# First layer's norm statistics moved to ScalarE, plain transposes of scaled rows, and an ordering edge on the scan's decay factors

## The chip, the core and the metric

The kernel runs on one core of one Trainium2 chip. The metric is the device time of one execution in microseconds (us); lower is better. Engines: PE is TensorE (PEld its weight loads), DVE is VectorE, ACT is ScalarE, POOL is GpSimd, and SP is SyncE, whose queue issues nearly all of the DMAs.

## The reference

Sixteen sequences (batches) of 512 tokens with 256 features, all in float32, pass through four residual layers: a state-space scan, a gated feed-forward layer whose operands go through a blockwise FP4 rounding, a linear attention, and the same feed-forward again. Each layer reads a layer norm of the running x.

```python
def _layernorm(x):                       # no gain, no bias
    return (x - mean(x)) / sqrt(var(x) + 1e-5)

# layer 1, per batch: d = 256 features, n = 16 states
x_in = xn @ w_in;  dt_low, Bm, Cm = split(x_in @ w_x)
dt = softplus(dt_low @ w_dt + b_dt) * 0.099 + 0.001
A = -exp(A_log)
for t in tokens:                         # the scan
    h = exp(dt[t] * A) * h + sum_d(dt[t] * A * u[t]) * Bm[t]
    y[t] = sum_n(h * Cm[t]) + Dp * u[t]
x = x + y
# layers 2 and 4: x + fp4_linear(silu(fp4_linear(xn, w_gate)) * fp4_linear(xn, w_up), w_down)
# layer 3: x + (causal linear attention with elu+1 features, 16 heads of 16) @ W_proj + b_proj
```

## The kernel before

**Tiling.** A batch is a tile `x` of 128 partitions by 4 chunks (`c`) by 256 features. Products want the features on the partitions, so each layer turns its normed tokens into `tT` (two halves `k` of 128 features by 512 tokens) through TensorE and copies the result out of PSUM on ScalarE.

**Stages.** Every batch passes through `scan` (layer 1: `prologue` for the next batch woven into `mamba` for this one), `ffn` 0 (tiles named `_f`), `attention`, and `ffn` 1 (`_g`). The stages are Python generators. Each `yield w` reports a weight, and `run_all` (L876) takes the stage whose pace is least, so that the scan of batch b, the first feed-forward of b-1, the attention of b-2 and the second feed-forward of b-3 are emitted interleaved. The constants `SCAN, FFN, ATTN` on L874 are the totals of the weights. The framework's scheduler then makes one queue for each engine out of the emitted program, by its own idea of durations; a queue is worked off in its order on the chip, and an instruction whose semaphore has not come holds everything behind it on that engine.

**The first layer's norm.** `front` (L446) computes the statistics: per chunk one `bn_stats` and one `bn_aggr` on DVE, then `inverse` (L400: a scale and shift on DVE, a power on POOL) gives `rstd`. The mean is never subtracted, because `centre` (L207) has taken it out of the weights. The three later norms get their statistics another way: the residual add on DVE leaves the row sum in `sums` (its `accum_out`), and `distances` (L394) squares x*(-256)+sum on ACT with the row sum in `dist`.

**`to_features`** (L422). Without `rstd` (the feed-forwards) it transposes with the identity, L429. With `rstd` (`front` and `attention`) it builds a diagonal matrix `diag` of one chunk's `rstd` on ACT (L435; two buffers, shared by both callers), and multiplies the raw rows by it on PE (L437), which transposes and scales at once: `x` is the stationary operand, `diag` the moving one.

**The scan.** `mamba` (L517) runs 16 steps for each batch. A step's decay factors live in one of `NBAR = 4` tiles `bar`. `spread` (L526) reads the step's dt from DRAM, broadcast over the 16 states, into a `bar` (L531, 511 KB, on SP's queue); it can start when the scan that last read that `bar` has ended. `decay` (L534) takes two exponentials and a square on ACT (L538, L541). The scan itself (L559) and the product with C (L563) are DVE's, the sum over the states (L569) is PE's. At step `at` the loop emits the decay of step `at + 1`, then the spread of step `at + 3`, then the scan of step `at`.

Names used later: L622 is the feed-forward's tanh on ACT, L623 and L624 the products behind it on DVE; L642 and L647 copy its transposed hidden tile `hqT` out of PSUM on ACT, and L651 is the down product on PE; L249 is the magnitude step of the FP4 rounding on ACT.

Of the kernel before, what the change touches and what calls it, by code (L numbers as in the profile page):

```python
# [10 lines left out]
F32 = mybir.dt.float32  # L11
BF16 = mybir.dt.bfloat16
AF = mybir.ActivationFunctionType
# [4 lines left out]
P = 128  # L18
# [14 lines left out]
def kernel(  # L33
# [385 lines left out]
            )  # L419
        return xn  # L420

    def to_features(pool, t, name, rstd=None):  # L422

        tT = pool.tile([P, ND, S], F32, tag="tT", name=f"tT_{name}", bufs=1)
        if rstd is None:
            for k in range(ND):
                pt = bank(f"pt_{name}_{k}")
                for c in range(NC):
                    nc.tensor.transpose(pt[:, ts(c, P)], t[:, c, ts(k, P)], ident)  # L429
                nc.scalar.copy(tT[:, k, :], pt)  # L430
            return tT
        pts = [bank(f"pt_{name}_{k}") for k in range(ND)]
        for c in range(NC):
            diag = small.tile([P, P], F32, tag="diag", name=f"diag_{name}_{c}")
            nc.scalar.activation(diag, ident, AF.Copy, scale=rstd[:, c : c + 1])  # L435
            for k in range(ND):
                nc.tensor.matmul(  # L437
                    pts[k][:, ts(c, P)], t[:, c, ts(k, P)], diag, start=True, stop=True
                )
        for k in range(ND):  # L440
            nc.scalar.copy(tT[:, k, :], pts[k])  # L441
        return tT
# [2 lines left out]

    def front(b, xt):  # L446

        stats = small.tile(
            [P, NC, nc.vector.BN_STATS_DIM], F32, tag="stats", name=f"st_m{b}"
        )  # L450
        mv = small.tile([P, NC, nc.vector.BN_AGGR_DIM], F32, tag="mv", name=f"mv_m{b}")
        for c in range(NC):
            nc.vector.bn_stats(stats[:, c, :], xt[:, c, :])
            nc.vector.bn_aggr(mv[:, c, :], stats[:, c, :])
        rstd = inverse(2, mv[:, :, 1], 1.0, f"m{b}")
        yield 2.4
        turned[b] = to_features(one, xt, f"m{b}", rstd)
        yield 1

    def prologue(b, xt):  # L460

        yield from front(b, xt)
        xnT = turned.pop(b)

        def from_xn(w, name):
            p = bank(f"{name}_{b}")
            for k in range(ND):
                nc.tensor.matmul(p, w[:, k], xnT[:, k, :], start=(k == 0), stop=(k == ND - 1))  # L468
            return p

        soft = one.tile([P, ND, S], F32, tag="soft", name=f"soft_{b}")
        dt = one.tile([P, ND, S], F32, tag="dt", name=f"dt_{b}")
        for e in range(ND):
            pz = from_xn(w_z_sb[:, :, ts(e, P)], f"pz{e}")
            nc.scalar.activation(soft[:, e, :], pz, AF.Abs, bias=b_dt_sb[:, e : e + 1])
            nc.scalar.activation(
                dt[:, e, :], pz, AF.Relu, bias=b_relu[:, e : e + 1], scale=DT_MAX - DT_MIN
            )  # L480
        yield 0.5
        nc.scalar.activation(soft, soft, AF.Tanh, scale=0.5)
        nc.scalar.activation(soft, soft, AF.Ln, bias=half_c, scale=0.5 * LN_C)
        nc.vector.scalar_tensor_tensor(dt, soft, DT_MIN - DT_MAX, dt, ALU.mult, ALU.add)

        dd = dram.tile([ND, 2, 32, 2, S], F32, tag="dt", name=f"dd_{b}")
        for e in range(ND):
            for q in range(4):
                nc.sync.dma_start(
                    dd[e, q // 2, :, q % 2, :], dt[32 * q : 32 * q + 32, e, :]  # L490
                )
        yield 1.5
        cm = one.tile([P, S], F32, tag="cm", name=f"cm_{b}", bufs=2)
        nc.scalar.copy(cm, from_xn(w_c_sb, "pcm"))
        yield 0.1

        while halfway[0] < b:
            yield 0
        u = one.tile([P, ND, S], F32, tag="u", name=f"u_{b}")
        for e in range(ND):  # L500
            nc.scalar.copy(u[:, e, :], from_xn(w_in_sb[:, :, ts(e, P)], f"pu{e}"))
        yield 0.5

        nc.vector.tensor_tensor(dt, dt, u, ALU.mult)
        pg = bank(f"pg_{b}")
        for k in range(ND):
            nc.tensor.matmul(
                pg, a_rep[:, k].rearrange("p n i -> p (n i)"), dt[:, k, :],
                start=(k == 0), stop=(k == ND - 1),
            )  # L510
        term = dt[:, 0, :]
        nc.scalar.copy(term, from_xn(w_b_sb, "pbm"))
        nc.vector.tensor_tensor(term, term, pg, ALU.mult)
        begun[b] = (u, dd, term, cm)
        yield 2

    def mamba(b, xt):  # L517
        u, dd, term, cm = begun.pop(b)

        inp = one.tile([P, 2, S], F32, tag="inp", name=f"inp_{b}")  # L520
        nc.scalar.copy(inp[:, 0, :], term)
        nc.gpsimd.tensor_copy(inp[:, 1, :], term)

        halves = small.tile([P, ND, NC], F32, tag="halves", name=f"halves_{b}")

        def spread(e, j, q0):  # L526

            bar = bars[state["bar"] % NBAR]
            state["bar"] += 1
            src = dd[e, q0 // 2, j * G8 : (j + 1) * G8, :, 1:S]  # L530
            nc.sync.dma_start(bar[:, :, 1:S], src.unsqueeze(0).to_broadcast([NS, G8, 2, S - 1]))  # L531
            return bar

        def decay(bar, e, j, q0):  # L534

            for i in range(2):
                g = 16 * e + 4 * (q0 + i) + j
                nc.scalar.activation(  # L538
                    bar[:, i, 1:S], bar[:, i, 1:S], AF.Exp, scale=a_col[:, g : g + 1]
                )  # L540
            nc.scalar.activation(bar[:, :, 1:S], bar[:, :, 1:S], AF.Square)  # L541
            return bar

        steps = [(e, j, q0) for e in range(ND) for j in range(4) for q0 in (0, 2)]
        sps = [spread(*steps[at]) for at in range(NBAR - 1)]
        ahead = decay(sps[0], *steps[0])
        for at, (e, j, q0) in enumerate(steps):
            bar = ahead
            if at + 1 < len(steps):
                ahead = decay(sps[at + 1], *steps[at + 1])  # L550
            if at + NBAR - 1 < len(steps):
                sps.append(spread(*steps[at + NBAR - 1]))
            if j == 0 and q0 == 0:
                py = ps_y.tile([P, S], F32, tag="y", name=f"py_{b}_{e}")
                nc.tensor.matmul(py, d_diag[:, e], u[:, e, :], start=True, stop=False)
                if e == ND - 1:
                    halfway[0] = b + 1
            h = one.tile([P, 2, S], F32, tag="hs", name=f"h_{b}_{e}_{j}_{q0}", bufs=3)
            nc.vector.tensor_tensor_scan(  # L559
                h.rearrange("p i t -> p (i t)"), bar.rearrange("p i t -> p (i t)"),  # L560
                inp.rearrange("p i t -> p (i t)"), 0.0, ALU.mult, ALU.add,
            )
            nc.vector.tensor_tensor(h, h, cm.unsqueeze(1).to_broadcast([P, 2, S]), ALU.mult)  # L563
            if q0 == 0:
                h0 = h
            else:

                for q in range(4):
                    nc.tensor.matmul(  # L569
                        py[32 * q : 32 * q + 32, :], red[:, j, :], (h0, h)[q // 2][:, q % 2, :],  # L570
                        start=False, stop=(j == 3),
                    )
            if j == 3 and q0 == 2:

                yT = one.tile([P, S], F32, tag="yT", name=f"yT_{b}_{e}")
                nc.scalar.copy(yT, py)
                pt = bank(f"pt_y_{b}_{e}")
                for c in range(NC):
                    nc.tensor.transpose(pt[:, ts(c, P)], yT[:, ts(c, P)], ident)
                for c in range(NC):  # L580
                    xc = xt[:, c, ts(e, P)]
                    nc.vector.scalar_tensor_tensor(
                        xc, pt[:, ts(c, P)], 1.0, xc, ALU.mult, ALU.add,
                        accum_out=halves[:, e, c : c + 1],
                    )
            yield 3.5

        stats["f", b] = sums, dist = summed(0, f"f{b}")
        nc.vector.tensor_tensor(sums, halves[:, 0, :], halves[:, 1, :], ALU.add)
        for c in range(NC):  # L590
            distances(xt, c, sums, dist)
        yield 2
# [80 lines left out]
    def attention(b, xs):  # L673
# [1 line left out]
        rstd = inverse(3, stats.pop(("a", b))[1], 1.0 / D**3, f"a{b}")  # L675
        stats["g", b] = summed(1, f"g{b}")
        yield 0.3
        xnT = to_features(att, xt, f"a{b}", rstd)
        yield 1


# [189 lines left out]
        nc.sync.dma_start(out[b].rearrange("(c p) d -> p c d", p=P), xs[b])  # L871


    SCAN, FFN, ATTN = 65.7, 40.2, 25.7  # L874

    def run_all(stages):  # L876

# [66 lines left out]
```

## Time and profile before

| | |
|---|---|
| median of 3 runs | 2773.36 us (2771.33 to 2779.51) |
| the profiled execution | 2774.32 us; span of its instructions 2772.6 us |
| DVE busy | 2432.1 us, 88% of the span |
| PE busy | 2418.5 us, 87% (PEld 1412.6 us, 51%) |
| ACT busy | 1504.5 us, 54% |
| POOL busy | 175.2 us, 6% |
| DMA | 165.00 MB, 60 GB/s over the span |
| granted TensorE clock | 0.942 of full speed |

Busy times of engines overlap; a row "line engine op out<-in xcount | busy, mean ns of one | idle before" says how long a group of instructions ran and how long its engine sat idle just before them, and what ended that. PE's busy time is modelled, and a float32 matmul shows as two records. Between about 700 and 2300 us the picture repeats with every batch: the store of dt to DRAM (L489) starts at 762.40 us for one batch and at 2226.07 us nine batches later, so a batch takes 162.6 us. After about 2450 us no scan is left, and only attention and feed-forward work of the last batches runs.

### The profile page before, as it was taken

The page shows a single profiled execution, that of the slowest core. Times are in us where ns is not written, and L with a number is a line of the kernel's source. Part 1 is how long each engine was busy: PE and PEld are TensorE (multiplying, and loading weights), DVE is VectorE, ACT ScalarE, POOL GpSimd, SP SyncE. Part 2 cuts the span into 40 slices and gives each one's busy share as a digit, 9 for nine tenths or more (in the row PEclk, how much of TensorE's full clock was granted, in tenths as well). Part 3 has the DMA queues.
Part 4 walks back from the last instruction along what each step waited for, and adds up shares of the span by engine and source line. Part 5 has one row for each costly group of instructions (what it writes and reads, how often), then busy time and mean ns, then how long its engine had stood idle before and what let it go on. Part 6 is the DMA issues. An engine that isn't in the chain of part 4 may idle for free.

```text
span 2772.6 us, 34094 instructions
## 1 busy us (share of the span) xinstructions
PE 2418.5 (87%) x12783; PEld 1412.6 (51%) x12783; DVE 2432.1 (88%) x3691; ACT 1504.5 (54%) x2910; POOL 175.2 (6%) x171
## 2 busy tenths in 40 slices
PE   5677889889898998989899898989989898898996
PEld 3134555455555555555555555545555554455664
DVE  7898898799899899989989999899999989887665
ACT  4776574465746556474555647455564645433332
POOL 2000000000001000000100000010000001000000
PEclk8788999999999999999999999999999999999998
DMA  5533222213113132221312232131322213200000
GB/s 144 129 99 84 61 54 50 73 46 91 46 38 88 42 80 50 78 60 38 84 46 77 53 77 61 39 84 41 81 54 65 73 38 73 50 1 8 8 1 15
DMA packets 97399, 165.00 MB, mean 60 GB/s; under 512 B 8689, under 2 KB 92626, under 8 KB 97234
## 3 DMA queue, kind: packets, MB, share of 16 engines
q1 hardware_dynamic: 95360, 161.77, 23.3%
q8 instruction: 100, 1.64, 0.3%
q10 hardware_dynamic: 1874, 1.06, 0.1%
q14 instruction: 65, 0.53, 0.1%
HBM read 146.02 MB, written 16.78 MB: 59 GB/s over the span
## 4 chain that ended last, share of the span: by engine, by line
DVE 39%; PE 37%; ACT 9%; DMA 8%; issue 4%; POOL 2%; SPq 0%; POOLq 0%; DVEq 0%; ACTq 0%
DVE h L559 15%; DMA bar<-dd 8%; PE pg_g L616 4%; PE pu_g L616 4%; DVE h L563 4%; PE po_g L651 4%; PE pg_f L616 3%; PE pu_f L616 3%; PE py L569 3%; ACT bar L538 2%; PE po_f L651 2%; DVE sm L736 2%; PE pz L468 2%; DVE v_f L245 2%; ACT bar L541 1%
## 5 line engine op out<-in xcount | busy, mean ns | idle before, releaser
L559 DVE TENSOR_TENSOR_SCAN h<-bar,inp 128x1024 f32<-128x1024 f32 x256 | 579.7, 2279 | 8.2 <-ACT bar L541 5.0
L538 ACT ACTIVATE bar<-bar,a_col 128x511 f32<-128x511 f32 x512 | 353.0, 717 | 319.6 <-DMA bar<-dd 291.9
L569 PE MATMUL py<-h,red 128*32 128x512 f32 x1024 | 295.8, 658 | 123.1 <-DVE h L563 122.0
L563 DVE TENSOR_TENSOR h<-h,cm 128x1024 f32<-128x1024 f32 x256 | 311.0, 1217 | 0.6
L541 ACT ACTIVATE bar<-bar 128x1022 f32<-128x1022 f32 x256 | 269.2, 1051 | 2.6
L651 PE MATMUL po_g<-wdT,hqT_g 128*128 128x256 f32 (+1 forms) x768 | 210.8, 420 | 36.8 <-ACT hqT_g L642 36.6
L651 PEld LDWEIGHTS po_g<-wdT,hqT_g 128*128 128x128 f32 (+1 forms) x768 | 146.7, 203 | 121.6 <-ACT hqT_g L642 70.4
L651 PE MATMUL po_f<-wdT,hqT_f 128*128 128x256 f32 (+1 forms) x768 | 198.5, 401 | 10.2 <-ACT hqT_f L642 10.2
L616 PE MATMUL pg_g<-wgT,tT_g 128*128 128x352 f32 x512 | 186.2, 486 | 0.8 <-DVE h_f L624 0.5
L651 PEld LDWEIGHTS po_f<-wdT,hqT_f 128*128 128x128 f32 (+1 forms) x768 | 137.5, 192 | 95.5 <-ACT hqT_f L647 29.0
L616 PE MATMUL pu_g<-wuT,tT_g 128*128 128x352 f32 x512 | 185.8, 487 | 0.3 <-DVE sm L736 0.3
L616 PE MATMUL pg_f<-wgT,tT_f 128*128 128x352 f32 x512 | 182.3, 479 | 0.1
L616 PE MATMUL pu_f<-wuT,tT_f 128*128 128x352 f32 x512 | 172.9, 460 | 4.5 <-DVE sm L736 2.7
L622 ACT ACTIVATE h_g<-pg_g 128x352 f32<-128x352 f32 x128 | 59.2, 462 | 209.5 <-PE pg_g L616 209.4
L736 DVE TENSOR_TENSOR sm<-psc,causal 128x512 f32<-128x512 f32 x256 | 163.9, 681 | 4.4 <-PE pn L760 3.5
L569 PEld LDWEIGHTS py<-h,red 128*32 128x32 f32 x1024 | 38.0, 111 | 227.2 <-DVE h L563 177.8
L774 POOL COPY dx<-den 128x256 f32<-128x256 f32 x64 | 42.3, 661 | 1435.3 <-PE pr L779 758.0
L249 ACT ACTIVATE big_f<-v_f 128x704 bf16<-128x704 f32 (+1 forms) x80 | 67.1, 839 | 119.1 <-DVE v_f L245 119.1
L616 PEld LDWEIGHTS pg_f<-wgT,tT_f 128*128 128x128 f32 x512 | 98.4, 198 | 65.4 <-issue 23.8
L616 PEld LDWEIGHTS pu_g<-wuT,tT_g 128*128 128x128 f32 x512 | 101.5, 201 | 58.9 <-issue 8.5
L623 DVE SCALAR_TENSOR_TENSOR h_g<-h_g,pg_g 128x352 f32<-128x352 f32 x128 | 65.0, 509 | 74.7 <-ACT h_g L622 74.6
L689 PE MATMUL pqk<-tT_a,w_qkv_sb 128*128 128x512 f32 x256 | 122.6, 616 | 8.2 <-ACT tT_a L441 8.2
(239 smaller groups left out, 4583.6 us busy)
## 6 DMA issues: line engine op xcount, KB each, us to landing
bar<-dd SPq DMA_DIRECT2D x256, 511.0 KB, 4.8
x<-in_L_attn_a_x_dram SPq DMA_DIRECT2D x16, 512.0 KB, 4.4
dd<-dt SPq DMA_DIRECT2D x128, 64.0 KB, 1.7
out_dram<-x SPq DMA_DIRECT2D x16, 512.0 KB, 4.9
w_qkv_sb<-in_L_attn_b_W_attn_dram ACTq DMA_DIRECT2D x1, 768.0 KB, 6.9
raw_d<-in_L_ffn_w_down_dram SPq DMA_DIRECT2D x1, 704.0 KB
raw_g<-in_L_ffn_w_gate_dram SPq DMA_DIRECT2D x1, 640.0 KB, 7.1
raw_u<-in_L_ffn_w_up_dram SPq DMA_DIRECT2D x1, 640.0 KB, 6.5
```

The costliest lines, as they stand in the source:

```text
L249: nc.scalar.activation(big, v, AF.Abs, scale=STEP)
L538: nc.scalar.activation(bar[:, i, 1:S], bar[:, i, 1:S], AF.Exp, scale=a_col[:, g : g + 1])
L541: nc.scalar.activation(bar[:, :, 1:S], bar[:, :, 1:S], AF.Square)
L559: nc.vector.tensor_tensor_scan(h.rearrange("p i t -> p (i t)"), bar.rearrange("p i t -> p (i t)"), inp.rearrange("p i t -> p (i t)"), 0.0, ...
L563: nc.vector.tensor_tensor(h, h, cm.unsqueeze(1).to_broadcast([P, 2, S]), ALU.mult)
L569: nc.tensor.matmul(py[32 * q : 32 * q + 32, :], red[:, j, :], (h0, h)[q // 2][:, q % 2, :], start=False, stop=(j == 3),)
L616: nc.tensor.matmul(pw[:, :HF], xqT[:, k, ts(c, P)], wT[:, k, cols], start=(k == 0), stop=(k == ND - 1),)
L622: nc.scalar.activation(hc, pg[:, :HF], AF.Tanh, scale=0.5)
L623: nc.vector.scalar_tensor_tensor(hc, hc, 1.0, pg[:, :HF], ALU.add, ALU.mult)
L651: nc.tensor.matmul(po[:, :D], hqT[:rows, r, :], wdT[:rows, r, :], start=(r == 0), stop=(r == NR - 1),)
L689: nc.tensor.matmul(pz, w_qkv_sb[:, k, ts(je, P)], xnT[:, k, :], start=(k == 0), stop=(k == ND - 1),)
L736: nc.vector.tensor_tensor(t, psc[g].rearrange("p (s t) -> p s t", t=P), causal.unsqueeze(1).to_broadcast([P, NH // 4, P]), ALU.mult,)
```

## The change

1. `front` takes no `bn_stats` and `bn_aggr` any more. For each chunk ACT runs a Copy with `accum_out` (the row sum) and then `distances`, as for the other norms; `inverse` divides by D**3. The weight of its first `yield` goes from 2.4 to 0.2, and `SCAN` from 65.7 to 63.5.
2. `to_features` with `rstd` scales whole rows (128x256) on ACT, chunk by chunk, into a tile `rows`, and PE transposes them with the identity. `rows` has no memory of its own: in `front` it shares the buffer of `soft`, in `attention` that of `ep`. The two `diag` buffers are gone.
3. In the scan, from the third step of a batch on, both exponentials of a step get an ordering edge behind the scan two steps ahead. The edge (`NoSync`) is one for the scheduler alone: it carries no semaphore, so it sets where the exponentials stand in ACT's queue and makes nothing wait on the chip by itself.

```diff
-    def to_features(pool, t, name, rstd=None):
+    def to_features(pool, t, name, rstd=None, tag=None):
 ...
+        rows = pool.tile([P, ND, S], F32, tag=tag, name=f"rows_{name}", bufs=1)
+        rows = rows.rearrange("p k s -> p (k s)")
         for c in range(NC):
-            diag = small.tile([P, P], F32, tag="diag", name=f"diag_{name}_{c}")
-            nc.scalar.activation(diag, ident, AF.Copy, scale=rstd[:, c : c + 1])
+            row = rows[:, ts(c, D)]
+            nc.scalar.activation(row, t[:, c, :], AF.Copy, scale=rstd[:, c : c + 1])
             for k in range(ND):
-                nc.tensor.matmul(
-                    pts[k][:, ts(c, P)], t[:, c, ts(k, P)], diag, start=True, stop=True
-                )
+                nc.tensor.transpose(pts[k][:, ts(c, P)], row[:, ts(k, P)], ident)
 ...
     def front(b, xt):
-        stats = small.tile(...)
-        mv = small.tile(...)
+        sums, dist = summed(0, f"m{b}")
         for c in range(NC):
-            nc.vector.bn_stats(stats[:, c, :], xt[:, c, :])
-            nc.vector.bn_aggr(mv[:, c, :], stats[:, c, :])
-        rstd = inverse(2, mv[:, :, 1], 1.0, f"m{b}")
-        yield 2.4
-        turned[b] = to_features(one, xt, f"m{b}", rstd)
+            nc.scalar.activation(squares, xt[:, c, :], AF.Copy, accum_out=sums[:, c : c + 1])
+            distances(xt, c, sums, dist)
+        rstd = inverse(2, dist, 1.0 / D**3, f"m{b}")
+        yield 0.2
+        turned[b] = to_features(one, xt, f"m{b}", rstd, "soft")
 ...
-        def decay(bar, e, j, q0):
+        def decay(bar, e, j, q0, behind=None):
             for i in range(2):
 ...
+                exp = nc.scalar.activation(bar[:, i, 1:S], bar[:, i, 1:S], AF.Exp, ...)
+                if behind is not None:
+                    tc.add_manual_dep(exp.ins, behind.ins.name, <NoSync>, reason="dt lands")
 ...
+        scans = []
         for at, (e, j, q0) in enumerate(steps):
             bar = ahead
             if at + 1 < len(steps):
-                ahead = decay(sps[at + 1], *steps[at + 1])
+                ahead = decay(sps[at + 1], *steps[at + 1],
+                              behind=scans[at - 1] if at >= 1 else None)
 ...
-            nc.vector.tensor_tensor_scan(
+            step = nc.vector.tensor_tensor_scan(
 ...
+            scans.append(step)
 ...
-        xnT = to_features(att, xt, f"a{b}", rstd)
+        xnT = to_features(att, xt, f"a{b}", rstd, "ep")
 ...
-    SCAN, FFN, ATTN = 65.7, 40.2, 25.7
+    SCAN, FFN, ATTN = 63.5, 40.2, 25.7
```

More of the change, by code (lines that the diff above doesn't have):

```diff
@@ L446, in front @@
     def front(b, xt):
[L448 to L451, printed above, removed]
+        sums, dist = summed(0, f"m{b}")
         for c in range(NC):
-            nc.vector.bn_stats(stats[:, c, :], xt[:, c, :])
-            nc.vector.bn_aggr(mv[:, c, :], stats[:, c, :])
-        rstd = inverse(2, mv[:, :, 1], 1.0, f"m{b}")
-        yield 2.4
-        turned[b] = to_features(one, xt, f"m{b}", rstd)
+            nc.scalar.activation(squares, xt[:, c, :], AF.Copy, accum_out=sums[:, c : c + 1])
[3 more added lines that the diff above has]
+        turned[b] = to_features(one, xt, f"m{b}", rstd, "soft")
         yield 1
@@ L469, in from_xn @@
             return p
-        soft = one.tile([P, ND, S], F32, tag="soft", name=f"soft_{b}")
+        soft = one.tile([P, ND, S], F32, tag="soft", name=f"soft_{b}", bufs=1)
         dt = one.tile([P, ND, S], F32, tag="dt", name=f"dt_{b}")
@@ L532, in spread @@
             return bar
-        def decay(bar, e, j, q0):
+        def decay(bar, e, j, q0, behind=None):
             for i in range(2):
                 g = 16 * e + 4 * (q0 + i) + j
-                nc.scalar.activation(
+                exp = nc.scalar.activation(
                     bar[:, i, 1:S], bar[:, i, 1:S], AF.Exp, scale=a_col[:, g : g + 1]
                 )
+                if behind is not None:
+                    tc.add_manual_dep(
+                        exp.ins, behind.ins.name,
+                        mybir.DependencyInfo(
+                            mybir.DependencyClass.NoSync, mybir.DependencyReason.DATA
+                        ),
+                        reason="dt lands",
+                    )
             nc.scalar.activation(bar[:, :, 1:S], bar[:, :, 1:S], AF.Square)
@@ L549, in mamba @@
             if at + 1 < len(steps):
-                ahead = decay(sps[at + 1], *steps[at + 1])
+                ahead = decay(
+                    sps[at + 1], *steps[at + 1],
+                    behind=scans[at - 1] if at >= 1 else None,
+                )
             if at + NBAR - 1 < len(steps):
```

## The prediction

> **What bounds the kernel now.** I read the page's busy times first, then its chain, then one steady stretch, then the waits, and last the chain in order of time.
>
> ```profile
> PE 2418.5 (87%) x12783; PEld 1412.6 (51%) x12783; DVE 2432.1 (88%) x3691; ACT 1504.5 (54%) x2910; POOL 175.2 (6%) x171
> DVE 39%; PE 37%; ACT 9%; DMA 8%; issue 4%; POOL 2%; SPq 0%; POOLq 0%; DVEq 0%; ACTq 0%
> ```
>
> Two engines are nearly full, and the chain changes between them. The odd entry is DMA with 8% of 2772.6 us, about 222 us, although the queues are mostly empty. A steady batch (columns: us, then PE, PEld, DVE, ACT, POOL busy) says the same without start and end:
>
> ```profile
> 727.00:886.00 159.00, 143.86 (x784) 84.22 (x784) 145.02 (x225) 91.89 (x178) 10.27 (x9) 0.97 0.26 63
> ```
>
> DVE is busy 91% of it, PE 90%, ACT 58%. So no more than 9% can come from waits here; the rest must be work taken off DVE and PE. The waits of all engines (total us, times, longest):
>
> ```profile
> ACT bar L538 <- DMA bar<-dd: 291.9, 149, 7.4
> DVE h_g L623 <- ACT h_g L622: 74.6, 60, 5.2
> DVE h_f L623 <- ACT h_f L622: 53.9, 35, 5.4
> PE po_g L651 <- ACT hqT_g L642: 36.6, 37, 3.0
> ACT diag_a L435 <- PE pt_a L437: 31.8, 28, 3.5
> ACT diag_m L435 <- PE pt_a L437: 18.6, 13, 2.2
> ```
>
> ACT stands 292 us before exponentials whose dt has not landed; DVE and PE stand behind ACT's tanh and copies. The chain shows how the first makes the second (start, us, what):
>
> ```profile
> 787.36 2.21 DVE h L559
> 789.59 4.86 DMA bar<-dd
> 794.49 0.05 issue
> 794.54 1.33 ACT bar L538 x2
> 795.87 0.48 ACT hqT_g L642
> 796.35 0.04 issue
> 796.39 3.85 PE po_g L651 x12
> ```
>
> A scan ends and frees a `bar`; its refill takes 4.86 us; two exponentials stand in ACT's queue for that refill, and the hidden tile's copy, which has nothing to do with them, stands behind them, and PE behind the copy. This comes about three times in each steady batch.
>
> **Part 1: the statistics.** What goes from DVE and what its nearest substitute costs on ACT:
>
> ```profile
> L453 DVE BATCH_NORM_STATS2 st_m<-x 128x6 f32<-128x256 f32 x64 | 24.3, 402 | 0.1
> L454 DVE BATCH_NORM_AGGREGATE mv_m<-st_m 128x2 f32<-128x6 f32 x64 | 10.3, 167 | 0.0
> L395 ACT ACTIVATE squares<-x,sum_g 128x256 bf16<-128x256 f32 x64 | 32.4, 506 | 19.0 <-DVE x L388 12.7 <-DVE half_g L236 5.5
> L395 ACT ACTIVATION_READ_ACCUMULATOR squares<-x,sum_g 128x1 f32 x64 | 12.1, 188 | 0.0
> ```
>
> DVE loses 24.3 + 10.3 = 34.6 us. DVE's time is its work plus its idle time, so this comes off in full unless idle time replaces it. ACT gains, for 64 chunks, two passes with accumulator: 2 x (32.4 + 12.1) = 89 us. ACT has 46% idle, which covers them; uncovered, they would cost up to 89. The new dependence is DVE's `var_m` (L403) waiting for the last `distances`; everything on DVE stands behind it. The other three norms have that wait already, and DVE lost 2.4 us to it in 48 times. Bounds 0 to 16 x 1.4 us (one chunk's two passes) = 22; I take 5. At the start POOL is busy with two powers of 5.4 us until 18 us and takes `rstd_m` only then, which hides batch 0's sums; batch 1's stand among ACT's setup copies in the built order: 0 to 5.6 us, I take 3. The yields fall together with `SCAN`, so the pace of the stages stays.
>
> The Trainium skill (ScalarE: Activation LUTs, Rules for kernel authors) speaks against this part: adds and multiplies belong on VectorE, not ScalarE. A chunk costs 0.57 us on DVE here and 1.39 us on ACT, so the trace agrees on the direction. By that rule the move would lose 64 x 0.82 = 52 us wherever ACT is what all wait for.
>
> **Part 2: rows and transposes.** Before and after by the nearest rows:
>
> ```profile
> L437 PE MATMUL pt_a<-diag_a,x 128*128 128x128 f32 x256 | 51.6, 366 | 14.0 <-ACT diag_a L435 13.8
> L437 PE MATMUL pt_m<-diag_m,x 128*128 128x128 f32 x256 | 37.3, 288 | 8.1 <-ACT diag_m L435 7.0 <-ACT wgT L313 0.7
> L429 PE MATMUL pt_f<-ident,xn_f 128*128 128x128 f32 x128 | 18.7, 292 | 2.7 <-DVE xn_f L253 2.5 <-ACT ep L696 0.2
> ```
>
> A product with `diag` shows as two records, a transpose as one: 128 products make 256 records in `pt_a`, while 128 transposes make 128 in `pt_f`. 256 products took 51.6 + 37.3 = 88.9 us; 256 transposes at 18.7/128 = 0.146 us take 37.4. PE loses 51.5 us. PE holds 37% of the chain, so I count 0.37 x 51.5 = 19 us; bounds 0 and 51.5. A scaled row is 128x256 with a scale by partition, like `ko` (L722, 499 ns) against `diag`'s 400: 128 x 0.1 = 13 us more on ACT, covered as above. In return no row waits for PE to hand back one of two `diag` buffers, 31.8 + 18.6 + 5.8 = 56 us of ACT's waits. Sharing buffers costs nothing: `soft` and `ep` were last read about 100 us before (L484 and L834 run near 1413 us, the next norm near 1540), and what writes them next needs `tT` anyway.
>
> At 1376 to 1380 us, where `pt_a` runs, the granted clock is 0.71 and `pt_a` takes 201 ns a record against 146 for `pt_m`; transposes of `pt_h_g` amid matmuls (1426 to 1429 us) have 1.00. The Trainium skill (TensorE: Matmul & The Clock Gate, Part 4: PE-mode transpose) says that transposes do not count as activity for releasing the clock. By that, part 2 would gain 256 x 0.055 = 14 us less of PE's time; the second window speaks against it for short runs of transposes.
>
> **Part 3: the ordering edge.** It carries no semaphore. In the built program the median count of ACT instructions between a step's refill and its first exponential goes from 5 to 18. To see whether that is enough I summed, for each step, the DVE work (by these rows' durations) that must have passed between the scan that frees the `bar` and the last DVE result that ACT has already waited for when it reaches the exponential. Where it is under 5.4 us (4.8 to land, 0.54 to issue) ACT may stand. That is so in 238 of 256 steps before and in 69 after, and what is missing sums to 938 and 197 us. ACT really stood 292; in proportion, 61 are left (estimate), so 79% go. Most of those left are steps 1, 6 and 9 of each batch.
>
> What it is worth is less than ACT's 292 or the chain's 222, since DVE mostly works meanwhile. I laid DVE's idle stretches between 100 and 2450 us (197 us) against ACT's 149 waits, each with the 3.5 us behind it (two exponentials, square, one more): 63 us coincide, and 119 of PE's 268. DVE's idle time is the one that adds to its work, so I take 0.79 x 63 = 50. Bounds: 0 (other waits fill the holes) and 119 (PE's).
>
> **The sum.** -34.6 (DVE work) - 50 (waits) - 19 (PE) + 5 (`var_m`) + 3 (start), and + 2.6 because ACT's 102 us more work is 7% more, taken on the 37 us that DVE waits for ACT's rounding step `big` (24.0 for L251 in `v_g`, 13.2 in `v_f`): -93. The profiled execution took 2774.3 us, 1.7 more than its span and 1 more than the median of the runs: 2681, so 2680.
>
> **Rivals.**
> *More than the sum.* Both full engines are relieved in the same places, and a queue in which ACT no longer stands lets PE run ahead as well. For it: PE's 119 us and the 56 us of waits for `diag`. Against: DVE's work alone is 2397 us, with about 15 idle at the start and 104 after 2450 us, so 2516 is the floor. With PE's 119 in place of the 50: 2681 - 69 = 2612.
> *Only the work goes.* ACT stands elsewhere instead: `h_g` already waits 209 us for PE's `pg_g`, which no edge changes. Then the 50 us stay: 2731; if PE's 19 stay too, 2750. This is also the case in which the edge does nothing on the chip.
> *Slower: the decay comes too late.* Exponentials queued behind the scan two ahead also stand behind ACT's waits for PE, and then the scan waits for the whole decay, 0.72 + 0.61 + 0.95 = 2.28 us of the chain. Before, the scan lost 5.0 us to ACT in all: the decays were far ahead. In the built program the DVE work between what ACT has waited for and the scan falls from a median of 24 to 12.5 us, and is under 5.6 in a sixteenth of the steps. It outweighs the gain once 93/2.28 = 41 of 224 steps wait in full; with 60 the time is 2680 + 137 = 2817. The 12.5 us speak against it.
> *Slower: ACT becomes the bound.* If all of ACT's 102 us lie on the chain, the time is 2680 + 102 = 2782; it decides from 93 us on. ACT's 58% in the steady batch speaks against it. The rule of the Trainium skill named in part 1 (ScalarE: Activation LUTs, Rules for kernel authors) would have it so.
>
> **How the numbers follow.** The sum 0.57, more 0.2, only work 0.14, too late 0.06, ACT bound 0.03. The time is that of the sum, 2680. The range, 2600 to 2755, takes in "more" and "only work" and leaves the two slower cases out, with part of the first rival's low tail. About 0.3% (8 us) is what a measurement of this kernel can tell from no change: faster 0.88, same 0.04 (the upper end of "only work", the lower of "too late"), slower 0.08.
>
> **What would show it.** ACT's wait for DMA before the exponentials near 60 us instead of 292, and DMA under 3% of the chain; DVE busy near 2397, PE near 2367, ACT near 1607; the rows of the tanh waits (74.6 and 53.9) down by a third; the scan's wait for ACT under 20 us; a batch in 156 to 157 us instead of 162.6. The prediction is wrong if the scan's wait for `bar` exceeds 90 us, or if DVE's idle time between 100 and 2450 us stays near 197 with the DMA waits gone.

## The result, and the profile after

The changed kernel takes 2725.68 us (median of 4 runs, 2721.27 to 2727.22) against 2773.54 us of the kernel before beside it: a ratio of 0.982, 95% interval 0.980 to 0.984. That is 48 us faster; 93 were forecast. The profiled execution took 2721.27 us with a span of 2719.5 us, 53.1 less than before. The page's busy times and its chain:

```profile
PE 2372.8 (87%) x12527; PEld 1379.8 (51%) x12527; DVE 2404.1 (88%) x3563; ACT 1560.4 (57%) x3166; POOL 216.5 (8%) x171
DVE 46%; PE 31%; ACT 10%; issue 6%; POOL 4%; DMA 2%; DVEq 0%; SPq 0%; POOLq 0%; ACTq 0%
```

DMA has nearly left the chain (8% to 2%), and POOL's share has doubled (2% to 4%). DVE is busy 28.0 us less, and the span less that busy time, DVE's idle time, goes from 340.5 to 315.4 us: 28.0 of work and 25.1 of idle time make the 53.1. The waits after (total us, times, longest):

```profile
ACT bar L537 <- DMA bar<-dd: 46.4, 22, 4.7
DVE h_g L635 <- ACT h_g L634: 39.1, 26, 5.2
DVE h_f L635 <- ACT h_f L634: 22.3, 21, 2.3
DVE x L388 <- PE pro L826: 28.5, 18, 2.5
DVE h L570 <- PE py L581: 27.5, 12, 2.9
PE py L581 <- DVE h L575: 76.8, 45, 6.7
PE pt_a L440 <- ACT rows_a L438: 71.8, 38, 5.1
```

The last four were not shown before, and stood there like this:

```profile
DVE x L388 <- PE pro L814: 8.7, 8, 1.9
DVE h L559 <- PE py L569: 2.1, 2, 1.4
PE py L569 <- DVE h L563: 122.0, 53, 7.1
PE pt_a L437 <- ACT diag_a L435: 13.8, 3, 6.2
```

ACT's wait for dt fell from 291.9 to 46.4 us, and with it DVE's two waits for tanh, from 128.5 to 61.4. At the same time DVE waits 45 us more for PE (`pro` and `py`); PE waits 58 us more for the scaled rows, and 45 us less for the scan's product (`py`). The steady stretch, in the columns of a window, between the stores of dt of the same nine batches; first before, then after:

```profile
762.40:2226.07 1463.67, 1327.79 (x7147) 776.38 (x7147) 1341.28 (x2053) 837.56 (x1621) 92.44 (x81) 0.97 0.25 62
```

```profile
741.55:2181.55 1440.00, 1302.01 (x7004) 763.65 (x7003) 1326.01 (x1981) 867.83 (x1765) 116.90 (x81) 0.95 0.25 63
```

A batch now takes 160.0 us instead of 162.6: 24 us of the gain are here, 21 before the seventh batch's store, 9 after the sixteenth's. In the steady stretch DVE lost 15 us of work and only 8 of idle time. The groups that the change made, and the power they wait for:

```profile
L440 PE MATMUL pt_a<-ident,rows_a 128*128 128x128 f32 x128 | 39.1, 421 | 73.2 <-ACT rows_a L438 71.8
L440 PE MATMUL pt_m<-ident,rows_m 128*128 128x128 f32 x128 | 22.3, 325 | 5.6 <-ACT rows_m L438 5.6
L451 ACT ACTIVATE squares<-x 128x256 bf16<-128x256 f32 x64 | 26.0, 406 | 1.6 <-DMA x<-in_L_attn_a_x_dram 1.1
L395 ACT ACTIVATE squares<-x,sum_m 128x256 bf16<-128x256 f32 x64 | 32.1, 501 | 0.9
L405 POOL TENSOR_TENSOR rstd_a<-var_a,neg_half 128x4 f32<-128x4 f32 x16 | 45.1, 2818 | 73.0 <-DVE var_a L403 73.0
```

The same power took 1924 ns on average before. Where the new wait lies is seen in one norm of the attention, in the chain in order of time:

```profile
1027.64 0.09 DVE var_a L403
...
1027.80 2.92 POOL rstd_a L405
...
1030.75 0.51 ACT rows_a L438
1031.26 0.49 ACT squares L395 x2
1031.75 0.40 ACT rows_a L438
1032.15 0.40 ACT squares L451 x2
1032.55 0.40 ACT rows_a L438
1032.94 0.49 ACT squares L395 x2
1033.44 0.40 ACT rows_a L438
1033.84 0.61 ACT bar L537
1034.45 0.55 ACT tT_a L442
...
1035.04 3.59 PE pqk L701 x4
```

Three things follow one another: a power of 2.92 us; the four scaled rows, with part 1's passes for the first layer's statistics between them; and an exponential ahead of the copy of `tT`, which now waits for nothing. PE stands until the first rows come, and then gets them in pairs; here is its timeline, with the idle time before each piece in brackets:

```profile
1031.31 0.69 PE L440 MATMUL pt_a<-ident,rows_a 128*128 128x128 f32 x2 [5.12 <-ACT rows_a L438]
...
1035.04 3.58 PE L701 MATMUL pqk<-tT_a,w_qkv_sb 128*128 128x512 f32 x4 [0.46 <-ACT tT_a L442]
```

5.12 us idle, and then four records of `pqk` (two products) in 3.58 us. At the same place before, PE had the scan's sums (`py`) to work on ahead of `pt_a` and between its groups, and twelve records of `pqk` took 5.42 us:

```profile
1048.98 1.92 PE L569 MATMUL py<-h,red 128*32 128x512 f32 x2 [3.99 <-DVE h L563]
...
1056.13 5.42 PE L689 MATMUL pqk<-tT_a,w_qkv_sb 128*128 128x512 f32 x12 [0.58 <-ACT tT_a L441]
```

### The profile page after: what moved, and what is told of

The parts are those of the page before. It is cut to its first block, busy times and chain, and to the rows that moved or that the text cites. A ratio compares the mean times of both kernels' runs of the same rounds, so it can differ in the third digit from the quotient of the medians.

```text
span 2719.5 us, 33632 instructions
## 1 busy us (share of the span) xinstructions
PE 2372.8 (87%) x12527; PEld 1379.8 (51%) x12527; DVE 2404.1 (88%) x3563; ACT 1560.4 (57%) x3166; POOL 216.5 (8%) x171
## 4 chain that ended last, share of the span: by engine, by line
DVE 46%; PE 31%; ACT 10%; issue 6%; POOL 4%; DMA 2%; DVEq 0%; SPq 0%; POOLq 0%; ACTq 0%
DVE h L570 11%; DVE h L575 5%; PE po_f L663 3%; PE pg_f L628 3%; PE pqk L701 3%; DVE sm L748 3%; PE pu_f L628 2%; PE pg_g L628 2%; DMA bar<-dd 2%; PE py L581 2%; DVE v_f L245 2%; PE pu_g L628 2%; PE po_g L663 2%; POOL rstd_a L405 2%; POOL rstd_f L405 2%
## 5 line engine op out<-in xcount | busy, mean ns | idle before, releaser
L570 DVE TENSOR_TENSOR_SCAN h<-bar,inp 128x1024 f32<-128x1024 f32 x256 | 580.5, 2279 | 35.9 <-PE py L581 27.5
L537 ACT ACTIVATE bar<-bar,a_col 128x511 f32<-128x511 f32 x512 | 347.8, 718 | 48.9 <-DMA bar<-dd 46.4
L581 PE MATMUL py<-h,red 128*32 128x512 f32 x1024 | 267.6, 673 | 76.8 <-DVE h L575 76.8
L663 PE MATMUL po_f<-wdT,hqT_f 128*128 128x256 f32 (+1 forms) x768 | 205.6, 412 | 13.2 <-ACT hqT_f L654 13.2
L663 PE MATMUL po_g<-wdT,hqT_g 128*128 128x256 f32 (+1 forms) x768 | 200.4, 404 | 14.7 <-ACT hqT_g L654 14.7
L663 PEld LDWEIGHTS po_g<-wdT,hqT_g 128*128 128x128 f32 (+1 forms) x768 | 138.9, 194 | 95.5 <-ACT hqT_g L659 36.9
L701 PE MATMUL pqk<-tT_a,w_qkv_sb 128*128 128x512 f32 x256 | 141.2, 700 | 7.0 <-ACT tT_a L442 7.0
L249 ACT ACTIVATE big_g<-v_g 128x704 bf16<-128x704 f32 (+1 forms) x80 | 67.6, 845 | 122.3 <-DVE v_g L245 122.1
L634 ACT ACTIVATE h_g<-pg_g 128x352 f32<-128x352 f32 x128 | 57.9, 460 | 129.7 <-PE pg_g L628 129.4
L654 ACT COPY hqT_f<-pt_h_f 128x512 f32<-128x512 f32 (+1 forms) x128 | 50.5, 424 | 135.8 <-PE pt_h_f L650 133.9
L628 PEld LDWEIGHTS pu_f<-wuT,tT_f 128*128 128x128 f32 x512 | 97.3, 190 | 54.7 <-DVE h_g L635 2.1
```

Source lines behind the costliest of these rows:

```text
L249: nc.scalar.activation(big, v, AF.Abs, scale=STEP)
L537: exp = nc.scalar.activation(bar[:, i, 1:S], bar[:, i, 1:S], AF.Exp, scale=a_col[:, g : g + 1])
L570: step = nc.vector.tensor_tensor_scan(h.rearrange("p i t -> p (i t)"), bar.rearrange("p i t -> p (i t)"), inp.rearrange("p i t -> p (i t)" ...
L581: nc.tensor.matmul(py[32 * q : 32 * q + 32, :], red[:, j, :], (h0, h)[q // 2][:, q % 2, :], start=False, stop=(j == 3),)
L628: nc.tensor.matmul(pw[:, :HF], xqT[:, k, ts(c, P)], wT[:, k, cols], start=(k == 0), stop=(k == ND - 1),)
L634: nc.scalar.activation(hc, pg[:, :HF], AF.Tanh, scale=0.5)
```

## The experiments

The kernel before ran beside every group; its median there was 2770.3 to 2774.3 us, and each ratio is against it.

### The three parts alone and in pairs

**Theories.** A: the ordering edge earns most, and the other parts give some of it back. B: only the work taken off earns. Six kernels have the remaining combinations of the three parts.

**edge_only**: part 3 on the kernel before.

```diff
-                ahead = decay(sps[at + 1], *steps[at + 1])
+                ahead = decay(sps[at + 1], *steps[at + 1],
+                              behind=scans[at - 1] if at >= 1 else None)
```

> Part 3 alone, on the kernel before: the ordering edge on the exponentials; statistics on DVE and the diagonal matmuls as before. Theory A (the edge earns most, and other parts give some of it back): ACT's wait for bar from DMA falls from 292 us to under 70, DVE's idle time between 100 and 2450 us falls by 40 to 60 us, and the time is 2715 to 2735 us. Theory B (only the work taken off DVE and PE earns; the holes that the edge closes open elsewhere): the wait for DMA falls as in A, but the time stays within 10 us of 2773.

2745.53 us, 0.990 (0.989 to 0.992). ACT's wait fell to 47.0 us as both theories had it, but both times are missed, and DVE's idle time between 100 and 2450 us fell by 13 us and not by A's 40 to 60.

**rows_only**: part 2 alone, on the kernel before.

```diff
-            diag = small.tile([P, P], F32, tag="diag", name=f"diag_{name}_{c}")
-            nc.scalar.activation(diag, ident, AF.Copy, scale=rstd[:, c : c + 1])
+            nc.scalar.activation(row, t[:, c, :], AF.Copy, scale=rstd[:, c : c + 1])
...
-                nc.tensor.matmul(pts[k][:, ts(c, P)], t[:, c, ts(k, P)], diag, start=True, stop=True)
+                nc.tensor.transpose(pts[k][:, ts(c, P)], row[:, ts(k, P)], ident)
```

> Part 2 alone: scaled rows and plain transposes for both callers; statistics on DVE, no edge. PE busy falls by 46 to 52 us in both theories. Theory A: 2745 to 2765 us (PE holds 37% of the chain before, 19 us). Theory B: all that the change earned comes from the work of parts 1 and 2, so here about half of the 48 us: 2745 to 2755.

2775.77 us, 1.001 (0.999 to 1.003): above both ranges, and PE's busy time fell by 21.6 us in place of 46 to 52.

**stats_only**: part 1 alone, on the kernel before.

```diff
-            nc.vector.bn_stats(stats[:, c, :], xt[:, c, :])
-            nc.vector.bn_aggr(mv[:, c, :], stats[:, c, :])
+            nc.scalar.activation(squares, xt[:, c, :], AF.Copy, accum_out=sums[:, c : c + 1])
+            distances(xt, c, sums, dist)
...
-        yield 2.4
+        yield 0.2
...
-    SCAN, FFN, ATTN = 65.7, 40.2, 25.7
+    SCAN, FFN, ATTN = 63.5, 40.2, 25.7
```

> Part 1 alone: sums and distances on ACT, SCAN 63.5, first yield 0.2; diagonal matmuls and no edge. DVE busy falls by 28 to 35 us in both theories. Theory A: ACT already stands 292 us for DMA, and 90 us more work in the same queue eats most of it: 2755 to 2780. Theory B: 2738 to 2748, the work of DVE in full.

2770.51 us, 1.000 (0.998 to 1.002), as A has it; DVE's busy time fell by 17.8 us, less than the 28 to 35 of both.

**rows_stats**: the changed kernel without the edge.

```diff
-                    behind=scans[at - 1] if at >= 1 else None,
+                    behind=None,
```

> Parts 1 and 2 without the edge (the changed kernel with no edge given). Theory A: ACT's wait for DMA is back at 250 to 300 us and the time 2750 to 2775. Theory B: the wait is back but the time stays at 2720 to 2735, as with the edge.

2799.56 us, 1.010 (1.008 to 1.011): slower than before, and above both ranges; ACT's wait is back at 233.5 us.

**edge_rows**: parts 2 and 3, which is rows_only with the edge of edge_only.

```diff
+                              behind=scans[at - 1] if at >= 1 else None)
```

> Parts 2 and 3 together, statistics still on DVE. The runs so far: the edge alone 0.990 of before, rows alone 1.001, statistics alone 1.000, rows and statistics 1.010, all three 0.982. Theory C (the work that each part takes off is small and is worth something only where the queues' order lets it; the edge repairs the order that parts 1 and 2 spoil): 2725 to 2740 us, more gained than by the edge alone. Theory D (the parts add up and the rest is chance of the order): the edge's 27 us and nothing more, 2740 to 2752.

2751.38 us, 0.993 (0.990 to 0.995): D's range, not C's.

**edge_stats**: parts 1 and 3, the changed kernel with `diag` put back.

```diff
-            nc.scalar.activation(row, t[:, c, :], AF.Copy, scale=rstd[:, c : c + 1])
+            diag = small.tile([P, P], F32, tag="diag", name=f"diag_{name}_{c}")
+            nc.scalar.activation(diag, ident, AF.Copy, scale=rstd[:, c : c + 1])
```

> Parts 1 and 3 together, with the diagonal matmuls. Theory C: 2720 to 2740 us, since DVE's 28 us of work come off once ACT does not stand for DMA. Theory D: 2740 to 2752 us.

2733.57 us, 0.987 (0.985 to 0.989): C's range, not D's.

All eight combinations side by side. The times are medians; the rest is from one profiled execution of each. DVE's idle time is the span less its busy time; the last three columns are ACT's wait for dt, PE's wait at `pt_a` for its operand, and PE's wait at `py` for the scan's product:

| parts | us (median) | DVE busy | DVE idle | ACT for dt | `pt_a` | `py` |
|---|---|---|---|---|---|---|
| none | 2773.5 | 2432.1 | 340.5 | 291.9 | 13.8 | 122.0 |
| rows | 2775.8 | 2432.0 | 336.7 | 327.9 | 9.7 | 136.1 |
| stats | 2770.5 | 2414.3 | 355.7 | 229.6 | 11.1 | 112.5 |
| rows, stats | 2799.6 | 2406.1 | 390.5 | 233.5 | 14.6 | 111.9 |
| edge | 2745.5 | 2425.1 | 318.5 | 47.0 | 98.0 | 72.5 |
| edge, rows | 2751.4 | 2423.1 | 319.8 | 36.0 | 76.4 | 71.9 |
| edge, stats | 2733.6 | 2415.1 | 314.3 | 86.1 | 77.3 | 73.1 |
| all | 2725.7 | 2404.1 | 315.4 | 46.4 | 71.8 | 76.8 |

What follows:

*The edge carries the gain.* In all four pairs the time falls: by 28 us alone, 24 with rows, 37 with stats and 74 with both. B falls, since rows and stats alone, which take the same work off, are at 1.001 and 1.000. A has the order right, the edge first, but its times for edge_only, rows_only and rows_stats are all missed. Of C and D neither holds: with the edge there, rows gain nothing more, as D has it, and stats do, as C has it. No theory here foretells what a part is worth beside the others.

*The edge brings DVE's idle time to 314 to 320 us, whatever else is changed.* Without it the idle time is 337 to 391. So its worth depends on what else is there: 22 us of idle time alone, 17 with rows, 75 with both other parts.

*With the edge PE's standing moves to `pt_a`.* In all four pairs that wait rises by 57 to 84 us, while PE's wait at `py` falls by 35 to 64. The edge does not only let ACT run on; it changes which work is queued where, and PE's standing moves from the scan's sum to attention's transposes or products with `diag`. This holds with `diag` and with `rows`, so part 2 did not make it. That this wait is what limits the gain is not shown. In which rows DVE then stands differs: with `rows` at `pro` and `py` (28.5 and 27.5 us in the changed kernel), in edge_only at the exponentials of attention, which come behind `pt_a` and `pqk`, and a copy of the first layer:

```profile
DVE qk L711 <- ACT ep L710: 46.4, 20, 5.7
DVE dt L513 <- ACT dt L512: 37.0, 13, 4.5
```

Before, these two stood at 23.4 and 4.3 us. The waits at `pro` and `py` do not come from the edge: rows_stats, without it and with only 14.6 us at `pt_a`, has most of them already.

```profile
DVE x L388 <- PE pro L826: 24.0, 20, 1.9
DVE h L570 <- PE py L581: 21.3, 17, 2.9
```

*Parts 1 and 2 lose 27 us together without the edge.* The waits of rows_stats show one possible reason:

```profile
ACT bar L537 <- DMA bar<-dd: 233.5, 139, 7.3
DVE h_f L635 <- ACT h_f L634: 83.0, 38, 5.5
DVE var_m L403 <- ACT squares L395: 18.6, 12, 2.2
```

The first layer's statistics are now ACT's, and ACT still stands 233 us for dt; DVE waits 18.6 us for them, against 2.0 in the changed kernel. That names 17 of the 75 us of idle time between these two kernels. It is not the whole reason: in stats_only ACT stands as long (229.6 us), and `var_m` is not among DVE's waits there. The tanh waits of both feed-forwards do not explain the loss either (113.2 us here, 128.5 before). What makes the rest of the 27 us is not settled.

### How late the decay may stand

**late_edge**: the decay of the next step is emitted behind the scan and ordered behind it, one step ahead instead of two.

```diff
+            if at + 1 < len(steps):
+                ahead = decay(sps[at + 1], *steps[at + 1], behind=step)
```

> The changed kernel with each decay emitted behind, and ordered behind, the scan one step ahead instead of two. The rival of the prediction (a decay that comes too late makes the scan wait for 2.28 us): the scan's wait for bar from ACT rises from 6 us to over 200 us in 224 steps, and the time to over 2850 us. If DVE's other work covers the decay even so: under 60 us of that wait, and 2720 to 2760 us. In both, ACT's wait for DMA goes under 46 us.

2758.59 us, 0.995 (0.994 to 0.997): the second reading, not the rival. **three_ahead**: behind the scan three steps ahead, from the fourth step of a batch on.

```diff
-                    behind=scans[at - 1] if at >= 1 else None,
+                    behind=scans[at - 2] if at >= 2 else None,
```

> The changed kernel with the edge behind the scan three steps ahead, the one whose bar is refilled next after the one in question, in place of two; from the fourth step on. With the other parts as in the change, no edge gave 2800 us, one step ahead 2759, two steps 2726. Theory C (the edge's worth is the cover that it gives the refill, against the lateness of the decay): ACT's wait for bar from DMA lies between the 46 us of two steps and the 234 us of none, at 80 to 160, and the time between 2735 and 2775. Theory G (a smaller delay keeps nearly all of the cover, since the refill takes only 4.7 us, and leaves the decay earlier): under 80 us of wait, and 2705 to 2726. If the order as a whole decides, the time need not follow the wait, as in the three runs before.

2747.07 us, 0.991 (0.989 to 0.993), as C has it. With no edge, three, two and one steps ahead ACT waits 233, 147, 46 and 16 us for dt, and the time is 2800, 2747, 2726 and 2759 us: the wait falls step by step, and the time is best at two. The runs under the next two headings move the time by as much with the order alone, so part of these steps may be that. What is longer at one step is seen in the waits of late_edge:

```profile
DVE qk L706 <- ACT ep L705: 55.6, 34, 7.4
DVE h L565 <- ACT bar L548: 14.5, 12, 4.8
PE pt_a L440 <- ACT rows_a L438: 111.0, 38, 7.9
```

The scan's own wait for its decay, the rival "too late" of the prediction, is 14.5 us. Larger are the waits of attention (25.3 and 71.8 in the changed kernel); that the order now puts its ACT work later would explain them, but no run tests it.

### The pace of the stages

**pace**: the changed kernel with the old total of weights, though the yield is 0.2.

```diff
-    SCAN, FFN, ATTN = 63.5, 40.2, 25.7
+    SCAN, FFN, ATTN = 65.7, 40.2, 25.7
```

> The changed kernel with SCAN back at 65.7 (the total of the yields stays 63.8), nothing else: all work is the same and only the interleaving of the stages shifts by 3%. Theory C: 2715 to 2740 us. Theory D (order alone moves the time by as much as the parts do): more than 15 us away from 2726, on either side.

2790.31 us, 1.007 (1.005 to 1.009), as D has it. One number, off by 3%, turns 48 us of gain into 20 of loss, while ACT's wait for dt stays at 37.1 us. So a short wait for dt is not enough for a gain, and any difference between two kernels here may hold some tens of microseconds that come from the order of the queues alone. Its steady window and the wait that took over:

```profile
741.58:2247.85 1506.27, 1371.94 (x7005) 795.09 (x7004) 1334.63 (x1980) 877.51 (x1765) 114.02 (x81) 0.94 0.23 60
```

```profile
DVE x L670 <- PE po_g L663: 56.6, 27, 6.2
```

The same work (x7005 records against x7004) takes PE 70 us longer, and DVE waits 35 us longer at `po_g`, of 62 us more idle time in all.

### What holds up the transposes

**rows_ahead**: attention emits its scaled rows and transposes ahead of its first yield, so that no other stage's instructions come between the power and the rows in the emitted program.

```diff
-        yield 0.3
         xnT = to_features(att, xt, f"a{b}", rstd, "ep")
-        yield 1
+        yield 1.3
```

> The changed kernel with attention's rows emitted ahead of its first yield (0.3 moved behind, the total the same). In the queue of ACT the four rows_a then have one pass of the next batch's sums between them and the copies, in place of four passes with their accumulators. Theory E (the sums between the rows hold up attention): PE's wait for rows_a falls from 72 us to under 30, time 2700 to 2718. Theory F: the wait falls, and the time stays within 8 us of 2726.

2753.57 us, 0.993 (0.991 to 0.995), with both theories missed. The transposes did become shorter, the wait before them did not. This is their group, with the mean and the wait:

```profile
L440 PE MATMUL pt_a<-ident,rows_a 128*128 128x128 f32 x128 | 30.0, 410 | 76.3 <-ACT rows_a L438 76.3
```

30.0 us against 39.1: in the changed kernel PE gets them in pairs as the rows come, here at once (14 waits instead of 38). edge_rows, where no sums exist, has 29.9, and rows_stats, where they do, 38.5. So the sums between the rows cost PE 9 us of busy time; but the wait in total is no smaller, and the whole is 28 us slower.

**power_first**: scan and product are ordered behind the latest powers on POOL, for the scheduler alone.

```diff
+            for late in (step, prod):
+                for power in state.get("pow", {}).values():
+                    tc.add_manual_dep(late.ins, power.ins.name, <NoSync>, reason="the power first")
```

> The changed kernel, with one more edge for the scheduler alone: scan (L570) and product (L575) of a step are ordered behind the powers on POOL that are emitted before them. In DVE's queue of the changed kernel the scan stood right behind var_a and var_f in 12 batches each and the product behind var_g; now small products (L416) stand behind var_a and the mean behind var_g, while var_f still has the scan. Theory E (the power lasts as long as the DVE instruction beside it, 1.0 us alone, 1.9 beside the product, 2.9 beside the scan, and attention waits for it): rstd_a and rstd_g go from 2.8 and 1.7 to 1.0 us mean, rstd_f stays 2.8, and the time falls by 10 to 30 us, to 2696 to 2716. Theory F (the power's time lies beside other work): the means fall as in E and the time stays within 8 us of 2726.

2903.45 us, 1.046 (1.044 to 1.048): the means fell as both theories had it, and both times are missed by far. **both**: rows_ahead and power_first together.

> Both edits of the two runs before together. Theory E: 2680 to 2705 us, the two gains added. Theory F: within 8 us of 2726. If the order as a whole weighs more than the one wait that an edit takes away, the three runs of this call do not add up, and differ from 2726 by over 15 us in either direction.

2915.24 us, 1.051 (1.049 to 1.053): the third reading, all three runs more than 15 us away. The powers of attention did become short, and PE's wait at `pt_a` fell from 71.8 to 34.6 us; these are power_first's group and its costliest PE wait:

```profile
L405 POOL TENSOR_TENSOR rstd_a<-var_a,neg_half 128x4 f32<-128x4 f32 x16 | 19.6, 1228 | 33.4 <-DVE var_a L403 33.4
```

```profile
PE py L590 <- DVE h L575: 249.9, 77, 8.5
```

But the scans now come late, and PE waits 250 us for their products instead of 77. So neither experiment prices the long power or the interleaved rows by themselves: each moved the order of all queues, and that weighed more. What those two cost in the changed kernel stays open. No kernel tried beats the changed one.

## Why the prediction was right in direction and nearly twice too large

**The mechanism of the edge held.** ACT's wait for dt was forecast at 61 us and is 46.4; DMA is at 2% of the chain (forecast: under 3%); the scan's wait for its decay is 6.2 us (under 20); the tanh rows fell by half (a third). `var_m` waits 2.0 us (5 in the sum), and the first store of dt starts 0.3 us later (42.87 to 43.19; 3 in the sum). A batch takes 160.0 us where 156 to 157 were forecast. That the time lay in the range says less: 155 us wide, the range would also have held edge_only, edge_rows and edge_stats.

**The term of the waits, -50, was mis-sized: -25 for all idle time, where -58 had been summed** (-50 - 19 + 5 + 3 + 2.6). The step that failed is "DVE's idle time is the one that adds to its work, so I take 0.79 x 63 = 50". The 63 us of coincidence were no price. Only 9 of them lie in ACT's 149 waits themselves, the others in the 3.5 us that were added behind each wait. Waits and additions cover 791 of the 2350 us between 100 and 2450 us, or 34%, and 34% of DVE's 197 us of idle time is 66: what chance alone would give (for PE, 90 of the 119). In the changed kernel the same count is 10 us, and 9 by chance, because 22 waits are left. So the fall from 63 to 10 says how many waits went, and not that 50 us were found. DVE's idle time in these 2350 us went from 197 to 177, by 20. By the prediction's own sign of being wrong, idle time that stays near 197 with the DMA waits gone, a third of the way was made to the 139 that the sum implies.

DVE's waits over the whole span say where: tanh -67, `po_g` -10, `big` of `v_g` -3; against `py` +25, `pro` +20, `dt` +6, `num` +5. The eight combinations show that with the edge PE's standing moves to `pt_a` and DVE's idle time stops at 314 to 320 us. They do not show that the one makes the other: of the 56.0 us at `pro` and `py` rows_stats has 45.3 without the edge. What sets the 314 to 320 us stays open. The prediction had 0 as the lower bound, "other waits fill the holes", but no estimate of how much they would fill. The 2.6 us that were added for `big` came out as 3 us less.

**DVE's work, -34.6, came to -28.0**, and of this only part is part 1's: the four pairs with and without it give -17.8, -25.9, -10.0 and -19.0, a mean of 18. The removed rows are gone in full, but a row's duration overlaps its neighbours': `var_a` at 1027.55 us lasts 0.17, and the scan behind it starts at 1027.62. Of the kernel before, the 128 short rows have only 24.0 us to themselves; in the rest of the 34.6 us a neighbour is busy too, so it stays when they go. The same on ACT: the new rows are 82.1 us for the statistics and 58.2 for the scaled rows in place of 48.0 for `diag`, 92 more, and busy time rose 56 (forecast 102).

**PE's term, -19 of 51.5, rested on transposes of 0.146 us.** `pt_m` took 174 ns each and `pt_a` 305, together 61.4 us against 88.9: 27.5 saved. Where nothing else was changed (rows_only) they took 28.8 + 18.1, 42.0 saved, and the time did not move (1.001). So PE's share of the chain was no price for PE's work here. PE's busy time did fall by 45.7 us, near the forecast, but that is luck: it came in part by other rows (`py` -28, `pqk` +19), whose modelled time depends on how they are queued. The Trainium skill (TensorE: Matmul & The Clock Gate, Part 4: PE-mode transpose), by which transposes do not release the clock, would have had 37 saved; the measured saving is below both. The mean clock of the profiled executions leans that way: 0.927 to 0.937 in the four kernels with transposes, 0.941 to 0.944 in the four with `diag`. But rows_only saved 42.0, more than 37, and the idle time before `pt_a` is an equally good reason for the rest.

**The rivals.** "Only the work goes" had 2731 us, nearer than the forecast, but by another way: it left the tanh waits in place, because `h_g` waits for `pg_g`, "which no edge changes"; that wait fell too (209.4 to 129.4 us). "ACT becomes the bound" did not come: part 1 alone is at 1.000, so the rule of the Trainium skill (ScalarE: Activation LUTs, Rules for kernel authors) that adds and multiplies belong on VectorE, which would have lost 52 us, did not decide where ACT was idle 44% of the time. "The decay comes too late" did not come at two steps; at one step the scan waited 14.5 us for its decay, so the loss there did not come by it either.

## What to carry to other kernels

An instruction that waits for a DMA in an in-order queue holds up everything behind it, and an ordering edge that costs nothing on the chip can remove that wait (292 to 46 us here, and a gain in all four pairs). What it is worth can't be read from the idle time of another engine that coincides with the waits, until that is compared with what chance would give: here 63 against 66. Work moved to an engine that stands in such waits earned nothing while they lasted (stats alone 1.000) and something after (0.987 against 0.990), so such parts should be tried together, though a change of order alone moves the time by more than that. Durations of short rows are no price for taking them out, and where a scheduler orders the queues, a pace constant can weigh more than the whole change (65 us against 48).

## What the runs showed of the hardware that was not expected

**A small power on POOL ends shortly after what DVE does beside it.** The same 128x4 instruction in the timeline of the kernel before, at two places:

```profile
1043.35 1.01 POOL L405 TENSOR_TENSOR rstd_g<-var_g,neg_half 128x4 f32<-128x4 f32 x1 [1.57 <-DVE mean_g L413]
...
1047.71 1.22 DVE L563 TENSOR_TENSOR h<-h,cm 128x1024 f32<-128x1024 f32 x1
1047.88 1.91 POOL L405 TENSOR_TENSOR rstd_a<-var_a,neg_half 128x4 f32<-128x4 f32 x1 [3.53 <-DVE var_a L403]
```

And in the changed kernel:

```profile
1027.62 2.29 DVE L570 TENSOR_TENSOR_SCAN h<-bar,inp 128x1024 f32<-128x1024 f32 x1
1027.80 2.92 POOL L405 TENSOR_TENSOR rstd_a<-var_a,neg_half 128x4 f32<-128x4 f32 x1 [3.66 <-DVE var_a L403]
```

1.01 us beside a reduction of a single operand (`amax_f`, from 1043.25 us on); 1.91 when DVE's product of two operands has started just before, 2.92 when it is the scan. Both times the power ends 0.8 to 0.9 us after DVE's instruction (1048.93 and 1029.91). The Trainium skill (SBUF — State Buffer, section "SBUF: two separate sides") states it: VectorE with two SBUF inputs and GpSimd take the port pair they share as an exclusive lock for a whole instruction. The trace agrees, for the scan with its two inputs (`bar` and `inp`) as for the product. The change made the scan follow `var_a` in place of the product, and POOL's busy time rose by 41 us, with the edge alone by 36.

**The clock after PE's idle time.** The window with the four slow records of `pqk` in the changed kernel (the granted clock is the third number from the end):

```profile
1035.00:1039.00 4.00, 3.96 (x9) 1.94 (x10) 4.00 (x4) 2.52 (x6) 0.73 (x1) 0.59 0.00 0
1039.00:1043.00 4.00, 4.00 (x14) 2.04 (x13) 3.04 (x4) 4.00 (x8) 0.00 (x0) 1.00 0.48 103
```

Before, at the same place:

```profile
1056.10:1060.00 3.90, 3.87 (x9) 1.82 (x10) 3.42 (x5) 2.21 (x5) 0.00 (x0) 1.00 0.50 134
```

After 5.12 us of idle time and eight transposes in short groups the clock is still at 0.59, and a record of `pqk` takes 895 ns (3.58 / 4) instead of 452 (5.42 / 12). Over the whole run `pqk` took 141.2 us instead of 122.6. In the eight combinations it took 129.1 to 142.1 us with the edge and 119.6 to 132.6 without, so in each pair this price comes with the edge, which also brings the wait at `pt_a`. The mean clock goes another way. It fell from 0.942 to 0.929, but edge_only, with the longest wait at `pt_a` (98.0 us), and edge_stats (77.3) stay at 0.941, while rows_stats, with 14.6, has 0.927. So the lower mean clock comes with the transposes in place of the products with `diag`, and not with that wait. Neither could be held by a sum over instruction durations of the kernel before.
